# A four-layer NCHW network on one core: the queue of layer 0's image loads, the place of the second image's statistics, and the order of layer 3's scores

## The chip, the cores and the metric

The kernel runs on one core of one Trainium2 chip. The metric is the device time of the whole program in microseconds (us). Engines are named as the profile names them: PE (matrix multiply), DVE (vector), ACT (activations), POOL (GpSimd), SP (the engine that here only issues transfers). Each engine executes its own instructions in the order in which they were written for it, and instructions wait for each other across engines by semaphores. A transfer is issued by SP, ACT or POOL, and stands in that engine's queue like any other instruction.

## The reference, cut to what matters

All values are float32. The input x has 8 images of 384 channels on 32 x 32 pixels. Four layers follow each other, each as a residual on a group norm:

```python
def _gn(v, G=32, eps=1e-5):            # 12 channels per group
    g = v.reshape(B, G, C // G, H, W)
    m = g.mean((2, 3, 4), keepdims=True); s = g.var((2, 3, 4), keepdims=True)
    return ((g - m) / sqrt(s + eps)).reshape(v.shape)

# layer 0: three branches q, k, v of 3x3 depthwise conv, batch norm, gelu, 1x1 conv
def _dwproj(x, dw, g, b, pw):
    y = gelu(_bn(depthwise3x3(x, dw), g, b))        # _bn: moments over images and pixels
    return einsum('oc,bchw->bohw', pw, y)
# then attention of 8 heads over 1024 tokens, a 1x1 conv and a batch norm
x = x + layer0(_gn(x))
x = x + layer1(_gn(x))   # 4 experts of two 1x1 convs, each token with its best two
x = x + layer2(_gn(x))   # ternary 3x3 depthwise conv and 1x1 conv
x = x + layer3(_gn(x))   # attention of 6 heads from 1024 tokens to 256 sampled keys, then a 1x1 conv
...
# layer 3, for each head: scores, softmax over the 256 keys, weighted values
attn = softmax(einsum('bhqd,bhkd->bhqk', q, k) * SCALE)
out  = einsum('bhqk,bhkd->bhqd', attn, v)
```

## The kernel before, in words

**Layer 0's convolution stage** takes roughly the first 365 us of the program. An image lies on 128 partitions in 3 chunks of 1024 pixels, and arrives as 3 transfers of 512 KB (`load_x`, which calls `load_image`; its transfers are recorded at L169). Five image buffers are shared by the eight images x0 to x7. x0 is loaded through SP's queue, x1 and x2 through POOL's (x2 held behind a transfer of the first image's stacks), and x3 to x7 through SP's, each when the norm of the image before it begins.

**The norm of an image** (`norm(b)`) has three steps. `begin` runs six `bn_stats` over the image on DVE (L104, two for each chunk) and one aggregate (L109). `middle` is a small matmul that averages over the group (`gna`, L115), followed on DVE by `ga` (L117) and `dm` (L120). `end` is a second small matmul (`gnb`, L126), then `ve` on DVE (L128), a power of minus one half on POOL (L96), the shift `ss` on DVE (L131), and three activations on ACT (L145) that write the scaled image into one of two padded buffers, `pads[b % 2]`. For the images that `ON_V` names (0, 2, 4 and 6) a copy `xn` of the padded chunk follows on DVE (L277), and 27 depthwise taps of one part of the channels on DVE as well (L299, L301), with statistics and a transfer out at the end of each of the three branches (`finish`, L306 to L309, the transfer `raw<-yv` issued by ACT).

**The convolution on PE** goes by 60 groups of channels (`work`), in the order of the images. For each group SP builds a tile `st` with 3 transfers of 168 KB from the padded buffer (L327, three rows of taps side by side on the partitions, ten such buffers), up to nine groups ahead (`AHEAD`). PE then runs 12 matmuls into two accumulation banks (L414; four banks in all, which the small matmuls of the norm share). ACT copies each bank out (L420), DVE takes its statistics (L422), and ACT issues 3 transfers of the result `raw` to DRAM (L437). A norm's three steps are written before three consecutive groups, some groups ahead of the first group that needs the image.

The order within an engine is fixed when the kernel is built: a scheduler walks over the program by the order in which things were written and its own estimate of when they are ready. `tc.issue_after(x)` keeps what is written under it behind instruction x. Transfers issued by POOL share eight completion slots, those by SP and ACT eight others, so that a ninth transfer waits for the first of its kind to land.

**Layer 3's attention** runs over six units for each image (three pairs of heads, two halves of the tokens). For a unit, `scores` multiplies q and k in two blocks (`s`, L1666: PE writes two PSUM tiles of 128 x 1024, of which there are two in all), each followed by its exponential on ACT (`p`, L1673). POOL adds the two blocks of p (`p01`, L1718), `weigh` multiplies p with the values (`pav`, L1682), and `sums` multiplies `p01` of the unit before with ones (`pss`, L1695), by which `divide` divides on DVE. Before, the scores of unit u+1 are written at the end of unit u. Tiles `p` and `p01` come from one pool of five buffers (`pl.flat`). For all images but the last, matmuls of layer 1 for other images (`y`, L1367) are mixed in between the units on PE; the last image has none beside it. A final 1x1 conv (`pf`, L1782) ends each image.

Of the kernel before, what the change touches and what calls it, by code (L numbers as in the profile page):

```python
# [8 lines left out]
AF = mybir.ActivationFunctionType  # L9
# [3 lines left out]
B, C, H, W = 8, 384, 32, 32  # L13
N = H * W
P = 128
KC = C // P
# [5 lines left out]
GC, NGC, GR, BR = 42, 9, 6, 4  # L22
# [31 lines left out]
def tile_kernel(ctx: ExitStack, tc: tile.TileContext, i: dict, out: bass.AP):  # L54
    nc = tc.nc
# [9 lines left out]
    def big(name):  # L65
        return ps_big.tile([P, N], F32, tag="big", name=name)
# [32 lines left out]
    def gn_start(x, tag, c, st):  # L99

        if st is None:
            st = small.tile([P, 2 * KC, 6], F32, tag="gn_st", name=f"st_{tag}")
        for h in range(2):
            nc.vector.bn_stats(st[:, 2 * c + h, :], x[:, c, h * HALF : (h + 1) * HALF])  # L104
        return st
# [119 lines left out]
    with ExitStack() as pa:  # L225
# [9 lines left out]
        pads = []  # L235
# [6 lines left out]
        xts = {}  # L242

        def load_x(b, queue=nc.sync):
            xts[b] = image(f"xa{b}")
            return load_image(xts[b], x_img[b], queue)
# [7 lines left out]
        cwr = load_a("cwr")  # L254
        vst = wa.tile([3 * GC, 3, 2, 6], F32, name="vst")

        def norm(b):

            xt, state = xts.pop(b), {}

            def begin():
                st = None
                for c in range(KC):
                    st = gn_start(xt, f"a{b}", c, st)
                state["st"], state["mv"] = st, gn_mean(st, f"a{b}")

            def middle():
                state["dm"] = gn_spread(state["mv"], f"a{b}", bank)

            def end():  # L270
                ss = gn_scale(*state["dm"], f"a{b}", bank)
                for c in range(KC):
                    dst = pads[b % 2][:, c, 1 : H + 1, :]
                    affine(dst, xt[:, c, :].rearrange("p (h w) -> p h w", h=H), ss)
                if b in ON_V:
                    xn = wa.tile([3 * GC, H, W], F32, tag="xn", name=f"xn{b}", bufs=2)
                    nc.vector.tensor_copy(xn, pads[b % 2][: 3 * GC, KC - 1, 1 : H + 1, :])  # L277
                    taps.extend(convolve(b, xn))
                for c in range(KC):
                    moments(xmv[:, b, c, :], state["st"][:, 2 * c : 2 * c + 2, :])  # L280

            return [begin, middle, end]
# [79 lines left out]
        begins, n = {}, -3  # L362
# [6 lines left out]
        def stacks(n):  # L369
            while later and len(work) - len(later) < n and later[0][0] in normed:  # L370
                sts[later[0]] = stack(*later[0])
                later.pop(0)
# [17 lines left out]
        for n, (b, g) in enumerate(work):  # L390
            if n in begins:
                b2 = begins[n]
                for k, f in enumerate(norm(b2)):
                    todo[n + k] = f, (b2 if k == 2 else 0)
                if b2 + 1 < B and b2 + 1 not in xts:
                    load_x(b2 + 1)
            if n in todo:
                f, b2 = todo.pop(n)
                f()
                normed.add(b2)  # L400
            stacks(n + AHEAD + 1)
            st = sts.pop((b, g))
            nch = GC if g < NGC else GR * BR
            y = ya.tile([3 * nch, N], F32, tag="y", name=f"y{b}_{g}")
            pk = [bank(f"pk{b}_{g}_{h}") for h in range(2)]
            steps = [(h, k) for h in range(2) for k in range(3)]
            if g == NGC:
                stl = wa.tile([3 * GR * BR, 2, 6], F32, tag="stl", name=f"stl{b}")
            for h, k in steps:
                dx, c0, c1, o0 = TAPS[k]  # L410
                rows = slice(h * (H // 2), (h + 1) * (H // 2))
                lhs = cw[:, g, dx, :] if g < NGC else cwr[:, dx, :]
                rhs = st[:, rows, c0:c1]
                nc.tensor.matmul(  # L414
                    pk[h].rearrange("p (h w) -> p h w", w=W)[: 3 * nch, :, o0 : o0 + c1 - c0],
                    lhsT=lhs, rhs=rhs, start=(k == 0), stop=(k == 2),
                )
                if k == 2:
                    hs = slice(h * HALF, (h + 1) * HALF)
                    nc.scalar.copy(y[:, hs], pk[h][: 3 * nch, :])  # L420
                    st1 = cst[:, g, 2 * b + h, :] if g < NGC else stl[:, h, :]
                    nc.vector.bn_stats(st1, y[:, hs])  # L422
            for k in range(3 * BR if g == NGC else 0):

                (j, v), r = divmod(k, 3), k * GR
                b1 = b + 1 - BR + j
                nc.gpsimd.dma_start(out=raw[v][b1, 3 * GC :, :, :], in_=y[r : r + GR, :])
                if v == 0:
                    nc.gpsimd.dma_start(
                        out=cst[: 3 * GR, NGC, 2 * b1 : 2 * b1 + 2, :],  # L430
                        in_=stl[r : r + 3 * GR, :, :],
                    )
            for v in range(3 if g < NGC else 0):
                to, of = raw[v][b, g % 3 : 3 * GC : 3, g // 3, :], y[v : 3 * GC : 3, :]

                queue = nc.gpsimd if b == B - 1 and g in (5, 6, 7) else nc.scalar
                queue.dma_start(out=to, in_=of)  # L437
            for _ in range(2):
                if taps:
                    taps.pop(0)()  # L440
            if b == B - 1:
                if g == 5:
                    load_b(0)
                for k in () if g == NGC else (g, NGC) if g == 5 else (g,):
                    bn_moments(cst, k, bn0)
# [49 lines left out]
    scale = HD0 ** (-0.5)  # L495
# [757 lines left out]
    def third(pl, k, name):  # L1253

        return pl.one([P, KC, HALF], f"hd{k}", name)
# [205 lines left out]
    def layer3(pl, b, xt, put, general):  # L1461
# [195 lines left out]

        def scores(pr, h):

            ps = []  # L1660
            for kc in range(2):
                nm = f"3_{b}_{pr}_{h}_{kc}"
                s = big(f"s{nm}")
                for j in range(2):
                    r = slice(64 * j, 64 * j + 64)
                    nc.tensor.matmul(  # L1666
                        s[:, j * HALF : (j + 1) * HALF],
                        lhsT=kt[r, pr, kc * P : (kc + 1) * P],
                        rhs=q[r, pr, h * HALF : (h + 1) * HALF],
                        start=True, stop=True,  # L1670
                    )
                p = pl.flat([P, N], f"p{nm}")
                nc.scalar.activation(p, s, AF.Exp, scale=0.125)  # L1673
                ps.append(p)
            return ps

        def weigh(pr, h, ps):
            pav = vbank(f"pav3_{b}_{pr}_{h}")
            for kc in range(2):
                for j in range(2):  # L1680
                    hd = 2 * pr + j
                    nc.tensor.matmul(  # L1682
                        pav[64 * j : 64 * j + 64, :], lhsT=vt[:, kc, hd * 64 : (hd + 1) * 64],
                        rhs=ps[kc][:, j * HALF : (j + 1) * HALF],
                        start=(kc == 0), stop=(kc == 1),
                    )
            return pav


        if not general:  # L1690
            def sums(u, p01):

                pss = fbank(f"pss3_{b}_{u}")
                for j in range(2):
                    nc.tensor.matmul(  # L1695
                        pss[64 * j : 64 * j + 64, :], lhsT=ones[:, :64],
                        rhs=p01[:, j * HALF : (j + 1) * HALF], start=True, stop=True,
                    )
                return pss
# [11 lines left out]
                )  # L1711


            ps, due3 = scores(*units[0]), None
            yield UNIT
            for u, (pr, h) in enumerate(units):
                p01 = pl.flat([P, N], f"p01_{b}_{u}")
                nc.gpsimd.tensor_tensor(p01, ps[0], ps[1], ALU.add)  # L1718
                pav = weigh(pr, h, ps)
                if due3:  # L1720
                    pss = sums(due3[2], due3[4])

                tu = pl.one([P, NG * LS], f"om{u % 2}", f"tu_{b}_{u}")[:, :HALF]
                tu = tu.rearrange("p (a b) -> p a b", b=32)
                nc.vector.transpose(tu.rearrange("p a b -> p (a b)"), pav)
                if due3:
                    divide(pss, *due3[:4])
                due3 = pr, h, u, tu, p01
                if u + 1 < NU3:
                    ps = scores(*units[u + 1])  # L1730
                yield UNIT
                yield 0.0
            divide(sums(due3[2], due3[4]), *due3[:4])
# [285 lines left out]
```

## Time and profile before

| | |
|---|---|
| median of 3 runs | 3647.08 us (3642.57 to 3647.95) |
| the profiled execution's own time | 3643.82 us |
| its span, first to last instruction | 3641.9 us |
| PE busy | 3533.7 us, 97% of the span |
| DVE, ACT, POOL busy | 48%, 35%, 6% |
| mean granted PE clock | 0.984 of full speed |
| SP's queue | 206.53 MB, 16.9% of the transfer engines' time |
| ACT's queue | 37.19 MB, 3.0% |
| POOL's queue | 6.44 MB, 0.6% |

A line of a timeline gives the start in us, the duration in us, the engine, the line of the kernel, the operation, output and inputs with their sizes, the number of instructions merged (x3), and in brackets the engine's idle time just before, with what ended it. A line of a table of waits gives the waiting engine and line, what it waited for, the total in us, how often, and the longest. A table by windows gives for each stretch each engine's busy time with its instructions, then the granted PE clock (1.00 is full speed), the share of the 16 transfer engines in use and the GB/s that they moved.

### The profile page before, as it was taken

Reading aid. Unit: us, or ns where it says so; the run is one execution under the profiler, and the core shown is the slowest. Engines: PE = TensorE matmul, PEld = TensorE weight load, DVE = VectorE, ACT = ScalarE, POOL = GpSimd, SP = SyncE. Lnnn points to the kernel's source line nnn. Section 1 sums busy time; section 2 is a strip of 40 time slices with the busy share of each in tenths; the row PEclk is TensorE's granted clock in tenths of the full one; section 3 lists DMA queues with packets and bytes.
Section 4 is the critical chain, followed back from the end, with each engine's and each line's share of the span. In section 5 each row is a group of like instructions: output and inputs, shape, how many; then the busy total and the mean of one; then the engine's idle time right before and its main releaser. Section 6 shows DMA issues by size and latency. Waiting matters only on the chain.

```text
span 3641.9 us, 38824 instructions
## 1 busy us (share of the span) xinstructions
PE 3533.7 (97%) x15533; PEld 1537.9 (42%) x15533; DVE 1752.0 (48%) x2808; ACT 1267.4 (35%) x1512; POOL 218.1 (6%) x201
## 2 busy tenths in 40 slices
PE   7999999999999999999899999999999999999888
PEld 3444343434343434344344444445344444444434
DVE  6776123232323232323346556374664647556663
ACT  2232554444444445434212321323322232322222
POOL 1101100000000000000000010200102010010112
PEclk9999999999999999999999999999999999999898
DMA  7767211111202020212430010111101001010000
GB/s 252 239 233 271 72 57 37 66 54 51 73 29 77 26 76 26 76 28 76 181 149 29 28 52 21 39 49 34 38 24 56 26 34 44 28 52 21 0 35 18
DMA packets 88893, 252.78 MB, mean 69 GB/s; under 512 B 19774, under 2 KB 20438, under 8 KB 88318
## 3 DMA queue, kind: packets, MB, share of 16 engines
q1 hardware_dynamic: 73972, 206.53, 16.9%
q10 hardware_dynamic: 12120, 37.19, 3.0%
q0 software_dynamic: 2608, 6.44, 0.6%
q8 instruction: 127, 2.08, 0.2%
q14 instruction: 66, 0.54, 0.1%
HBM read 133.44 MB, written 75.59 MB: 57 GB/s over the span
## 4 chain that ended last, share of the span: by engine, by line
PE 47%; DVE 2%; ACT 1%; POOL 1%; issue 0%; DMA 0%; DVEq 0%; POOLq 0%; ACTq 0%
PE ph L1346 14%; PE y L1367 14%; PE pq L1487 3%; PE pw L1450 3%; PE pf L1782 3%; PE s L1666 2%; PE pav L1682 2%; PE pk L1640 1%; PE pss L1695 1%; PE pv L1649 1%; PE xsb L1626 1%; PE plog L1096 1%; DVE off L1557 1%; DVE y L1442 1%; POOL p L1718 1%; ACT p L1673 1%
## 5 line engine op out<-in xcount | busy, mean ns | idle before, releaser
L696 ACT ACTIVATE p<-s 128x1024 f32<-128x1024 f32 x512 | 496.4, 1021 | 371.6 <-PE s L689 371.3
L704 PE MATMUL pav<-p,vt 64*64 64x512 f32 x4096 | 495.5, 589 | 0.0
L1367 PE MATMUL y<-hd,w_sb 128*128 128x512 f32 x1080 | 488.6, 600 | 3.5 <-DVE hd L1332 3.5
L1346 PE MATMUL ph<-h,w_sb 128*128 128x512 f32 x1104 | 485.2, 595 | 0.1
L689 PE MATMUL s<-qk,qk 48*64 48x512 f32 x3072 | 370.7, 593 | 0.0
L414 PE MATMUL pk<-st,cw_sb 126*126 126x512 f32 x720 | 314.7, 598 | 12.3 <-DMA st<-pad 11.6
L1346 PEld LDWEIGHTS ph<-h,w_sb 128*128 128x128 f32 x1104 | 208.0, 190 | 258.9 <-issue 255.1
L1367 PEld LDWEIGHTS y<-hd,w_sb 128*128 128x128 f32 x1080 | 200.2, 191 | 246.5 <-issue 236.0
L704 PEld LDWEIGHTS pav<-p,vt 64*64 64x64 f32 x4096 | 171.4, 133 | 270.6 <-issue 266.7
L665 DVE COPY ta<-pav 128x512 f32<-128x512 f32 (+1 forms) x65 | 44.2, 682 | 475.3 <-PE pav L704 475.3
L1442 DVE SCALAR_TENSOR_TENSOR y<-h,tap,y 128x961 f32<-128x961 f32 (+1 forms) x192 | 233.5, 1239 | 0.6
L1356 ACT ACTIVATE hd<-ph,b_sb 128x512 f32<-128x512 f32 x180 | 122.6, 681 | 311.1 <-PE ph L1346 311.1
L414 PEld LDWEIGHTS pk<-st,cw_sb 126*126 126x126 f32 x720 | 137.9, 193 | 178.4 <-issue 175.1
L1557 DVE SCALAR_TENSOR_TENSOR off<-q,dw_sb,off 128x225 f32<-128x225 f32 (+3 forms) x432 | 212.2, 546 | 1.6
L689 PEld LDWEIGHTS s<-qk,qk 48*64 48x64 f32 x3072 | 113.3, 133 | 220.7 <-issue 199.1
L79 DVE COPY qk<-pq 128x512 f32<-128x512 f32 x48 | 33.2, 692 | 265.4 <-PE pq L604 265.4
L1673 ACT ACTIVATE p<-s 128x1024 f32<-128x1024 f32 x96 | 93.2, 1021 | 189.3 <-PE s L1666 189.2
L420 ACT COPY y<-pk 126x512 f32<-126x512 f32 (+1 forms) x124 | 70.4, 584 | 227.2 <-PE pk L414 112.0
L1332 DVE TENSOR_TENSOR hd<-hd,cb 128x512 f32<-128x512 f32 x180 | 122.2, 684 | 41.1 <-ACT hd L1356 40.8
L1718 POOL TENSOR_TENSOR p<-p,p 128x1024 f32<-128x1024 f32 x48 | 113.0, 2354 | 369.1 <-ACT p L1673 369.1
L1782 PE MATMUL pf<-att,wp_sb 128*128 128x512 f32 x288 | 130.0, 607 | 4.3 <-DVE att L1709 3.7
L604 PE MATMUL pq<-g,wq_sb 128*128 128x512 f32 x288 | 129.7, 601 | 2.5 <-DMA wq_sb<-in_wq_dram 2.5
(296 smaller groups left out, 3856.2 us busy)
## 6 DMA issues: line engine op xcount, KB each, us to landing
g<-raw SPq DMA_DIRECT2D x72, 512.0 KB
st<-pad SPq DMA_DIRECT2D x180, 168.0 KB
raw<-y ACTq DMA_DIRECT2D x171, 168.0 KB
xh<-in_x_dram SPq DMA_DIRECT2D x48, 256.0 KB
f<-in_x_dram SPq DMA_DIRECT2D x24, 512.0 KB
f<-o SPq DMA_DIRECT2D x24, 512.0 KB
o<-ot SPq DMA_DIRECT2D x42, 256.0 KB
x<-in_x_dram SPq DMA_DIRECT2D x21, 512.0 KB
```

Of the source, the lines that this page charges most:

```text
L414: nc.tensor.matmul(pk[h].rearrange("p (h w) -> p h w", w=W)[: 3 * nch, :, o0 : o0 + c1 - c0], lhsT=lhs, rhs=rhs, start=(k == 0), stop=(k = ...
L604: nc.tensor.matmul(pq, lhsT=w_in[v][:, c, pr * P : (pr + 1) * P], rhs=acts[b][v][:, c, h * HALF : (h + 1) * HALF], start=(c == 0), stop=(c ...
L689: nc.tensor.matmul(s[64 * k : 64 * k + 64, j * HALF : (j + 1) * HALF], lhsT=kt[r, k0 : k0 + 64], rhs=qt[r, h * HALF : (h + 1) * HALF], sta ...
L696: nc.scalar.activation(p, s, AF.Exp, scale=scale)
L704: nc.tensor.matmul(pav[k][64 * j : 64 * j + 64, :], lhsT=vts[b % 2][r, kc, 2 * hd : 2 * hd + 2, :].rearrange("p a b -> p (a b)"), rhs=p[r, ...
L1346: nc.tensor.matmul(ph, lhsT=w1[:, e, c, dc * P : (dc + 1) * P], rhs=state["h1"][c], start=(c == 0), stop=(c == KC - 1),)
L1367: nc.tensor.matmul(y, lhsT=w2[:, e, dc, m * P : (m + 1) * P], rhs=state[h, k], start=(k == 0), stop=(k == NE * KC - 1),)
L1442: nc.vector.scalar_tensor_tensor(d, f, tap2[:, c, t : t + 1], d, ALU.mult, ALU.add)
L1557: nc.vector.scalar_tensor_tensor(d, f, dw3[:, t : t + 1], d, ALU.mult, ALU.add)
L1673: nc.scalar.activation(p, s, AF.Exp, scale=0.125)
L1718: nc.gpsimd.tensor_tensor(p01, ps[0], ps[1], ALU.add)
L1782: nc.tensor.matmul(pf[:, hs], lhsT=wp3[:, pr, m * P : (m + 1) * P], rhs=att[:, pr, hs], start=(pr == 0), stop=(pr == NPAIR3 - 1),)
```

## The change

There are three parts. The first writes the six statistics of image 1 (`begin` of `norm(1)`) under `issue_after` of image 0's copy `xn`, so that they stand behind it on DVE. The second takes the loads of x3 to x7 off SP's queue, and issues each on POOL's queue, in the text of the program right behind the `end` of the norm of the image before. The third splits layer 3's `scores` in its matmuls (`scores`) and its exponentials (`exps`): the matmuls of unit u+1 are written ahead of the `weigh` of unit u, and the exponentials behind `weigh` and `sums`; for the last image the exponentials too stand ahead of `weigh`, and their outputs lie in other tiles (`third`, four tiles, `hd0` to `hd3`, that layers 1 and 2 use earlier).

```diff
+        first_pad = []
         def norm(b):
             xt, state = xts.pop(b), {}
             def begin():
                 st = None
-                for c in range(KC):
-                    st = gn_start(xt, f"a{b}", c, st)
+                with tc.issue_after(first_pad[0].ins) if b == 1 else nullcontext():
+                    for c in range(KC):
+                        st = gn_start(xt, f"a{b}", c, st)
...
-                    nc.vector.tensor_copy(xn, pads[b % 2][: 3 * GC, KC - 1, 1 : H + 1, :])
+                    first_pad.append(
+                        nc.vector.tensor_copy(xn, pads[b % 2][: 3 * GC, KC - 1, 1 : H + 1, :])
+                    )
...
-                if b2 + 1 < B and b2 + 1 not in xts:
-                    load_x(b2 + 1)
             if n in todo:
                 f, b2 = todo.pop(n)
                 f()
                 normed.add(b2)
+                if 1 < b2 < B - 1:
+                    load_x(b2 + 1, nc.gpsimd)
...
         def scores(pr, h):
-            ps = []
+            ss = []
             for kc in range(2):
-                nm = f"3_{b}_{pr}_{h}_{kc}"
-                s = big(f"s{nm}")
+                s = big(f"s3_{b}_{pr}_{h}_{kc}")
...
-                p = pl.flat([P, N], f"p{nm}")
-                nc.scalar.activation(p, s, AF.Exp, scale=0.125)
+                ss.append(s)
+            return ss
+
+        def exps(u, ss):
+            ps = []
+            for kc in range(2):
+                nm = f"p3_{b}_{u}_{kc}"
+                if last:
+                    p = third(pl, 2 * (u % 2) + kc, nm).rearrange("p a n -> p (a n)")[:, :N]
+                else:
+                    p = pl.flat([P, N], nm)
+                nc.scalar.activation(p, ss[kc], AF.Exp, scale=0.125)
                 ps.append(p)
             return ps
...
-            ps, due3 = scores(*units[0]), None
+            ps, due3 = exps(0, scores(*units[0])), None
             yield UNIT
             for u, (pr, h) in enumerate(units):
                 p01 = pl.flat([P, N], f"p01_{b}_{u}")
                 nc.gpsimd.tensor_tensor(p01, ps[0], ps[1], ALU.add)
+                nxt = scores(*units[u + 1]) if u + 1 < NU3 else None
+                if last and nxt:
+                    nxt = exps(u + 1, nxt)
                 pav = weigh(pr, h, ps)
                 if due3:
                     pss = sums(due3[2], due3[4])
+                if nxt:
+                    ps = nxt if last else exps(u + 1, nxt)
...
-                if u + 1 < NU3:
-                    ps = scores(*units[u + 1])
                 yield UNIT
```

## The prediction

> **What bounds the kernel now.** First the page: PE is busy for 97% of the span, so only its gaps can be won. Then the chain that ended last and the groups: nothing but PE carries weight. So the table of PE's waits up to 460 us, then the timelines around the gaps.
>
> ```profile
> PE 3533.7 (97%) x15533; PEld 1537.9 (42%) x15533; DVE 1752.0 (48%) x2808; ACT 1267.4 (35%) x1512; POOL 218.1 (6%) x201
> ```
>
> The table of waits names the engine and line, what it waited for, the sum in us, how often, and the longest:
>
> ```profile
> PE gna_a L115 <- DVE mv_a L109: 16.8, 3, 9.1
> PE pk L414 <- DMA st<-pad: 11.6, 1, 11.6
> PE pmove L466 <- DVE rest L460: 5.3, 1, 5.3
> PE gna_a L115 <- DVE xmv L142: 3.6, 1, 3.6
> ```
>
> The convolution stage waits in two places: at the start for the first stacks, later for statistics of images (5.42 us at 175.99, 2.31 at 257.55, and 3.58 at 85.39; the 9.1 is the first image's load, which stays).
>
> ```profile
> 11.15 0.56 POOL L96 TENSOR_TENSOR ss_a<-ve_a,mhalf 128x1 f32<-128x1 f32 x1 [2.19 <-DVE ve_a L128]
> 11.79 1.28 DVE L104 BATCH_NORM_STATS2 st_a<-xa 128x6 f32<-128x512 f32 x2 [0.71 <-DMA xa<-in_x_dram]
> ...
> 16.19 0.10 DVE L131 SCALAR_TENSOR_TENSOR ss_a<-ga_a,ss_a 128x1 f32<-128x1 f32 x1
> 16.33 3.50 ACT L145 ACTIVATE pad<-xa,ss_a 128x1024 f32<-128x1024 f32 x3 [10.42 <-DVE ss_a L131]
> ...
> 22.46 6.07 PE L414 MATMUL pk<-st,cw_sb 126*126 126x512 f32 x9 [11.59 <-DMA st<-pad]
> ```
>
> And of PE alone at the later gaps:
>
> ```profile
> 85.39 0.56 PE L115 MATMUL gna_a<-mv_a,g_sb 128*128 128x2 f32 x2 [3.58 <-DVE xmv L142]
> 85.81 8.06 PE L414 MATMUL pk<-st,cw_sb 126*126 126x512 f32 x12
> ...
> 175.99 0.56 PE L115 MATMUL gna_a<-mv_a,g_sb 128*128 128x2 f32 x2 [5.42 <-DVE mv_a L109]
> ```
>
> POOL's power is done at 11.71, but the shift `ss` comes at 16.19: image 1's six statistics stand between, and everything of image 0 hangs on it. The group after the gap at 85.39 takes 8.06 us, where one takes 5.1 later.
>
> ```profile
> 40.00:50.00 10.00, 9.52 (x23) 4.07 (x22) 5.08 (x9) 4.41 (x7) 0.00 (x0) 1.00 0.92 319
> 60.00:85.00 25.00, 21.82 (x52) 9.43 (x51) 20.08 (x28) 7.81 (x12) 0.00 (x0) 0.99 0.83 282
> 85.00:90.00 5.00, 4.61 (x7) 2.27 (x8) 4.22 (x10) 0.00 (x0) 0.00 (x0) 0.50 0.73 251
> ```
>
> These windows show transfer engines at 0.92 while x2 loads, at 0.83 later, and PE's clock at 0.50 after the gap.
>
> **What the Trainium skill says.** "TensorE: Matmul & The Clock Gate", section "What's actually happening": after an idle window of about 3.4 us PE runs at half clock for about as long. The trace agrees: 0.50, and 8.06 - 5.1 = 3.0 us lost; the groups behind the gaps at 175.99 and 257.55 took 7.15 and 6.98, so 2.1 and 1.9 lost. "DMA: Bandwidth & Descriptors", section "Queues, rings and completion order": each transfer engine goes round its queues packet by packet, so another queue shares bandwidth and adds none. In the first window three queues add up to 319 GB/s at 0.92, 347 at most, which fits. "Perfetto Trace Analysis", section "DMA Instruction — SWDGE (GPSIMD)": what the profile shows on POOL is the making of descriptors, not the moving. x2's three take 1.63 us from 37.02, and DVE sees the data at 42.91, 45.89 and 48.38: it agrees.
>
> **Part 1, the statistics of image 1.** `ss` moves from 16.19 to about 11.8, behind POOL's power: -4.4 us for the scaled image, `st`, PE's first group and everything up to group 5. The 4.3 us of statistics are now behind the copy `xn` (19.87 + 0.69, less 4.4), where DVE idles 6.55 us before 27.91: cost nothing; without that cover 4.3 us of DVE ahead of taps that nobody waits for.
>
> **Part 2, the loads.** 15 issues leave SP, 15 join POOL. SP's slots are cheap there (stacks are issued 5 to 8 us ahead of PE in groups 3 to 8). On POOL nothing is queued but the powers of the norms. But the built order differs from the text: nothing ties a load to the norm it is written behind, and POOL's queue reads ss_a1, x2, x3, x4, x5, two chunks of x6, and only then the power of image 2, the third chunk, x7. All are asked for from 37.02 - 4.4 = 32.6 us on, at POOL's 0.54 us each (1.63 / 3); x5 needs x0's buffer (free by then), x6 x1's (free at about 37), and at most eight are in flight. DVE follows: image 2's `dm` stands behind the statistics of x4's second chunk's first half, its `ve` behind x5's first chunk, its `ss` behind x5's second, image 3's `ve` behind x7.
>
> So the time of one load, r, decides. Bounds: x1 alone moved at 281 GB/s (5 us of the trace), 524 KB in 1.9 us; x2 beside SP's 82 and ACT's 34 GB/s got 214, 2.45 us; DVE saw it every 2.7. I take 2.4: PE will stall here, and a stalled PE asks for less. Then, with landings at 38.5, 41.5, 44.0 (before, less 4.4) and each r later:
> - x4's second chunk lands at 44 + 5 x 2.4 = 56.0, `dm` of image 2 at 57.0; PE reaches `gnb` at 56.2 - 4.4 = 51.8: 5.3 us idle, some 2 of slow clock.
> - x5's second chunk lands at 63.2, with 1.3 of statistics `ss` comes at 64.6 (before 57.46). ACT's three activations and the copy queued behind them end at 70.2, PE's group 8 waits for that bank (before 66.1).
> - DVE's taps of image 2's part end at 86.9 (before about 72), since statistics stand among them. ACT's transfer of that result waits, and holds the bank copies queued behind it to 90.1; PE's group 11 is held there.
> - `ve` of image 3 is made at 101.8, `ss` at 103.4 (before 96.88), ACT's scaling ends at 108.7, and group 14 starts at 109.3 (before 103.6), some 2 of slow clock with it: +5.7 + 2 = +8 us against before, part 1's gain and the loss of 6.6 at 85.39 counted in.
>
> Images 5 and 7 are in their buffers long before their norms: -(5.42 + 2.1) - (2.31 + 0.65 + 1.9) = -12.4. Parts 1 and 2 together -4.4. The same replay gives +3.3 at r = 1.9, so 9.4 us for each us of r, and +9.9 at 2.75; above that I keep 9.4, since 8 loads after x2 stand ahead of image 2's `ss` and 15 ahead of image 3's `ve`.
>
> **Part 3, layer 3.** A unit of images 0 to 5 takes 7.4 us on PE (scores 1.92, fill of layer 1 2.77, values 1.87, sums 0.86) and has no gap except at the last unit, 0.27 and 0.49 an image. Scores earlier, exponentials later: the second exponential now waits for a buffer that `pss` frees; ACT's two take 2 x 1.02 us under 2.77 of fill. I take 0, bounds -2 and +4 with the stretch from 3440 to 3545 us, where DVE leads. The last image has no fill:
>
> ```profile
> 3588.93 1.08 PE L1682 MATMUL pav<-p,vt 128*64 128x512 f32 x4 [1.50 <-ACT p L1673]
> ...
> 3594.30 1.08 PE L1682 MATMUL pav<-p,vt 128*64 128x512 f32 x4 [0.32 <-ACT p L1673]
> ...
> 3617.85 1.08 PE L1695 MATMUL pss<-p,ones 128*64 128x512 f32 x4 [0.49 <-POOL p L1718]
> ```
>
> Its gaps are 1.50 + 2 x 0.32 + 0.27 + 2 x 0.26 + 0.49 = 3.4. With scores a unit ahead each exponential has 1.87 more to hide in; only the last sum on POOL (2.35) stays: -2.8.
>
> **The sum.** -4.4 + 0 - 2.8 = -7.2 us on the profiled execution's 3643.8: 3636.6. That execution was 3.3 below the median of 3647.08, so the forecast for the median is 3639.9, rounded 3640. What a measurement can tell from no change here is about 0.2%, 7.3 us: it sits on that edge.
>
> **Rivals.**
> (a) Loads faster, or DVE's statistics never late. At 281 GB/s the sum is +3.3 - 12.4 - 2.8 = -12: 3635. If no new wait appears at all, 4.4 + 12.4 + 2.8 = 19.6 are gained: 3627. For it: 281 was measured. Against: stacks and results were not moving then.
> (b) The reverse: POOL's queue gets the leavings. The window from 60 to 85 moved 282 GB/s at 0.83, so 340 in full; a group's six transfers of 172 KB in 5.1 us need 202, which leaves 138, and r = 3.8; three queues that all have work and share evenly leave 113, and r = 4.6. The sum passes zero at 2.4 + 7.2 / 9.4 = 3.2 us a load (165 GB/s), is slower by 7.3 from 3.95 on, and at 4.3, between the two, stands at +10.7: 3658. For it: SP, without image loads in its queue, runs ahead and asks for more. Against: PE's own stalls cut that demand.
> (c) No difference: r between 2.7 and 3.9 gives back at 50 to 110 us what images 5 and 7 return, 3643 to 3654, as r = 3.2 gives 3647. The place of the loads in the text would make no difference.
> (d) The scores of unit u+1 hold PSUM tiles that the fill wants, or wait for ACT: up to +4 in part 3, on top of any of these.
>
> **How the numbers follow.** My own case 0.36 (own range 3632 to 3648, half of it on each side of the edge), (a) 0.23, (b) 0.25, (c) with (d) 0.16. Faster 0.18 + 0.23 = 0.41; same 0.18 + 0.16 = 0.34; slower 0.25. The range leaves out the far end of (a) and the worst of (b): 3629 to 3659.
>
> **What would show it.** Step 1: `ss` of image 0 near 11.8, PE's first group near 18. Step 2: on POOL fifteen transfers ahead of image 2's power; DVE seeing a load every 2.4 us; PE idle 5 us before image 2's `gnb`; no wait at images 5 and 7. Part 3: no wait of `pav` in the last image. The forecast is wrong if r is far from 2.4, if PE waits for `st` between 40 and 90 us (stacks crowded out), or if layer 3's units grow beyond 7.4 us.

## The result, and the profile after

| | before | after |
|---|---|---|
| median | 3644.54 us (3638.92 to 3649.73, 15 runs) | 3636.39 us (3632.90 to 3639.65, 15 runs) |
| span of the profiled execution | 3641.9 us | 3634.6 us |

The ratio of after to before is 0.9976, with a 95% interval of 0.9969 to 0.9982: about 8.7 us faster (6.6 to 11.3). The forecast was 7.2 us. The two profiled executions differ by 7.3 us. PE is as full as before, and the fifteen transfers moved from SP to POOL show in POOL's count of instructions (201 before, 216 now). The page's first part, of the changed kernel:

```profile
PE 3528.1 (97%) x15533; PEld 1531.5 (42%) x15533; DVE 1766.5 (49%) x2808; ACT 1269.3 (35%) x1512; POOL 225.5 (6%) x216
```

Where PE waited in the first 460 us of the changed kernel (engine and line, what it waited for, sum in us, times, longest):

```profile
PE gna_a L115 <- DVE mv_a L109: 9.5, 2, 9.0
PE pk L421 <- DMA st<-pad: 9.4, 3, 7.6
PE gnb_a L126 <- DVE dm_a L120: 8.8, 2, 8.1
PE pmove L473 <- DVE rest L467: 5.3, 1, 5.3
PE pk L421 <- DVE ga_a L117: 3.0, 3, 2.5
```

The wait for the first stacks fell from 11.6 to 7.6 us. The waits of images 5 and 7 for their statistics are gone from the first line (16.8 before; of the 9.5 that stay, 9.0 are the first image's load and 0.5 image 2's). In their place stands a wait of 8.1 us for image 2's `dm`.

The timeline of the changed kernel's start:

```profile
11.07 0.56 POOL L96 TENSOR_TENSOR ss_a<-ve_a,mhalf 128x1 f32<-128x1 f32 x1 [2.13 <-DVE ve_a L128]
11.67 0.16 DVE L131 SCALAR_TENSOR_TENSOR ss_a<-ga_a,ss_a 128x1 f32<-128x1 f32 x1 [0.68 <-POOL ss_a L96]
11.86 3.50 ACT L145 ACTIVATE pad<-xa,ss_a 128x1024 f32<-128x1024 f32 x3 [6.03 <-DVE ss_a L131]
15.40 0.69 DVE L282 COPY xn<-pad 126x1024 f32<-126x1024 f32 x1 [3.57 <-ACT pad L145]
16.01 3.65 DVE L104 BATCH_NORM_STATS2 st_a<-xa 128x6 f32<-128x512 f32 x6
18.42 2.04 PE L421 MATMUL pk<-st,cw_sb 126*126 126x512 f32 x2 [7.63 <-DMA st<-pad]
```

The shift is made 0.04 us after POOL's power, image 1's six statistics run behind `xn` with nobody waiting, and PE's first group starts at 18.42 where it started at 22.46.

POOL's own timeline shows the hoisted loads:

```profile
32.80 4.22 POOL L169 DMA_DIRECT2D xa<-in_x_dram  x8
39.81 0.53 POOL L169 DMA_DIRECT2D xa<-in_x_dram  x1 [2.79 <-DMA xa<-in_x_dram]
43.72 0.53 POOL L169 DMA_DIRECT2D xa<-in_x_dram  x1 [3.38 <-DMA xa<-in_x_dram]
46.30 0.53 POOL L169 DMA_DIRECT2D xa<-in_x_dram  x1 [2.06 <-DMA xa<-in_x_dram]
49.19 0.53 POOL L169 DMA_DIRECT2D xa<-in_x_dram  x1 [2.36 <-DMA xa<-in_x_dram]
52.97 0.53 POOL L169 DMA_DIRECT2D xa<-in_x_dram  x1 [3.25 <-DMA xa<-in_x_dram]
56.24 0.53 POOL L169 DMA_DIRECT2D xa<-in_x_dram  x1 [2.75 <-DMA xa<-in_x_dram]
66.56 0.56 POOL L96 TENSOR_TENSOR ss_a<-ve_a,mhalf 128x1 f32<-128x1 f32 x1 [9.79 <-DVE ve_a L128]
```

Eight loads go out at once, and each further one when one has landed. So this queue is a clock for landings: 39.81 to 56.24 is 5 landings, 3.3 us each. Image 2's power comes only at 66.56, behind fourteen loads. It did not wait for them in POOL's queue: DVE made the `ve` that it needs at 66.27. What is late is DVE.

The table by windows shows the transfer engines meanwhile (the last two numbers are their share in use and the GB/s):

```profile
40.00:56.00 16.00, 12.05 (x29) 4.83 (x27) 9.26 (x20) 1.75 (x3) 2.45 (x5) 1.00 1.03 354
56.00:62.00 6.00, 0.00 (x0) 0.00 (x0) 4.56 (x13) 1.07 (x2) 0.53 (x1) 0.81 0.95 380
```

They are full, and stay so while PE stands still.

PE's timeline of the changed kernel, first where image 2 waits, then at the first small matmuls of images 4 and 5:

```profile
62.45 0.59 PE L126 MATMUL gnb_a<-dm_a,g_sb 128*128 128x1 f32 x2 [8.15 <-DVE dm_a L120]
...
147.34 0.28 PE L115 MATMUL gna_a<-mv_a,g_sb 128*128 128x2 f32 x2
...
178.42 0.28 PE L115 MATMUL gna_a<-mv_a,g_sb 128*128 128x2 f32 x2
```

Image 4's first small matmul stood at 139.32 before: 8.0 us late. Image 5's stood at 175.99 behind a gap of 5.42; now there is no gap, and 2.4 us are left of the delay. Matmul by matmul, the rest of the account of the two profiled executions is: -4.9 us at the end of the convolution stage (`pmove` 366.99 to 362.12), kept until layer 1; back to -1.9 after layer 3's images 0 to 5 (at 3440 us); -3.8 at the sampling of the last image (3564.35 to 3560.51); -8.8 at its final 1x1 conv (3618.86 to 3610.07); and -7.3 at the end of the program, since 8.7 us pass from the last matmul to the end where 7.2 passed before.

All this is one execution of each kernel, and executions of one and the same code spread. Four traces have the old convolution stage (the kernel before and three of the experiments): image 4's first small matmul stands in them at 138.7 to 142.7, and `pmove` at 367.0 to 371.2. The changed stage has a second trace below, with 150.4 and 365.2. A difference of 4 us between two single traces of this stage is therefore no finding by itself.

The last image, changed kernel, PE's timeline:

```profile
3583.95 2.04 PE L1672 MATMUL s<-q,kt 64*128 64x512 f32 x8 [1.21 <-ACT p L1689]
...
3610.07 2.41 PE L1801 MATMUL pf<-att,wp_sb 128*128 128x512 f32 x5
```

From the first unit's scores to the final conv there is one wait, 1.21 us, before the second unit's scores, and no other.

### The profile page after: what moved, and what is told of

It is laid out like the page before. It is cut to its first block, busy times and chain, and to the rows that moved or that the text cites. A ratio compares the mean times of both kernels' runs of the same rounds, so it can differ in the third digit from the quotient of the medians.

```text
span 3634.6 us, 38829 instructions
## 1 busy us (share of the span) xinstructions
PE 3528.1 (97%) x15533; PEld 1531.5 (42%) x15533; DVE 1766.5 (49%) x2808; ACT 1269.3 (35%) x1512; POOL 225.5 (6%) x216
## 4 chain that ended last, share of the span: by engine, by line
PE 40%; DVE 9%; ACT 1%; DMA 1%; POOL 0%; issue 0%; DVEq 0%; ACTq 0%; POOLq 0%
PE y L1374 11%; PE ph L1353 9%; DVE y L1449 5%; PE pq L1494 3%; PE pw L1457 3%; PE pf L1801 3%; PE s L1672 2%; PE pav L1698 2%; DVE hd L1339 1%; PE pk L1647 1%; PE pv L1656 1%; DMA o<-o 1%; PE pss L1711 1%; PE xsb L1633 1%; PE plog L1103 1%; DVE off L1564 1%
## 5 line engine op out<-in xcount | busy, mean ns | idle before, releaser
L1457 PE MATMUL pw<-y,upw 128*128 128x512 f32 x288 | 130.0, 605 | 4.1 <-DVE y L1449 4.1
```

The lines of the kernel that those rows point to most:

```text
L1457: nc.tensor.matmul(pw[h], lhsT=upw2[:, c, m * P : (m + 1) * P], rhs=y[c][:, hs], start=(c == 0), stop=(c == KC - 1),)
```

## The experiments

The theory to test was the forecast's own: the three parts add up, part 2 costs early what it returns late, because statistics that wait for hoisted loads stand in front of the norms on DVE. All differences below are (ratio - 1) times some 3644 us, with the interval of the ratio.

**Each part alone.**

Part 1 and part 2 alone are the diffs shown above without the other parts.

> The kernel before with part 1 alone (image 1's statistics behind the copy xn). My theory: the stage starts 4.4 us earlier and nothing takes it back, -4.4 us (-3.5 to -5). Rival, part 1 is absorbed: the wait of PE at 85 us ends with the load of x3 on SP's queue, and if that load does not come earlier the wait grows by what the start gained: 0, and the gap before image 3's first small matmul grows from 3.6 to about 8.

Measured: ratio 0.9988 (0.9982 to 0.9995), -4.4 us (-6.6 to -1.8). The gap before image 3's small matmul is 3.4 us in its trace (3.6 before), so nothing is taken back there: the load of x3 on SP's queue comes earlier as well, since what stands ahead of it in that queue does. The rival falls.

> The kernel before with part 2 alone (x3 to x7 on POOL's queue). My theory: the late norms of images 2 and 3 cost about what images 5 and 7 return, 0 us (-2 to +3): a wait of 5 to 8 us before image 2's second small matmul, some 12 us behind by 130 us, even by 270 us. Rival, the loads carry the whole gain of the change: -8 us.

Measured: ratio 1.0000 (0.9992 to 1.0009), 0 us (-2.9 to +3.3). In its trace image 4 is 16 us late, and 3 us are left at the end of the stage. Part 2 by itself buys nothing.

> The kernel before with part 3 alone. My forecast: -2.8 us, all of it in the last image. From the trace of the changed kernel: the last image gains 4.9, images 0 to 5 lose about 3, the stretch before the last image returns 1.8: -2 to -4. Rival, layer 3's order does nothing to the time: 0.

Measured: ratio 1.0003 (0.9995 to 1.0011), +1.1 us (-1.8 to +4.0). The expected -2.8 lies outside the interval. In the trace the last image gains 4.2 us from its sampling to its final conv, the part of the program before it loses 3.0, and 1.3 us are left. PE's waits between 2000 and 3300 us in this kernel:

```profile
PE ph L1346 <- ACT h L1295: 5.4, 5, 1.5
PE pw L1450 <- DVE y L1442: 0.9, 5, 0.2
```

and in the kernel before:

```profile
PE pss L1695 <- POOL p L1718: 3.0, 6, 0.5
PE pav L1682 <- ACT p L1673: 1.6, 6, 0.3
```

The old waits at the end of each image are gone, 4.6 us. In their place come 6.3 us: a pair of layer 1's matmuls (`ph`) has been scheduled one step earlier, ahead of the scaled image that ACT makes for it, and waits 5.4 us, and the matmuls of `pw` wait 0.9.

Part 3 for the last image alone:

```diff
-                nxt = scores(*units[u + 1]) if u + 1 < NU3 else None
-                if last and nxt:
-                    nxt = exps(u + 1, nxt)
+                nxt = None
+                if last and u + 1 < NU3:
+                    nxt = exps(u + 1, scores(*units[u + 1]))
...
                 due3 = pr, h, u, tu, p01
+                if not last and u + 1 < NU3:
+                    ps = exps(u + 1, scores(*units[u + 1]))
```

> The kernel before with part 3 for the last image alone; for images 0 to 6 scores and exponentials stand where they stood before. If the new order costs images 0 to 5 some 3 us, this is faster than part 3 alone by about 3, at -5 us. Rival, the loss seen there belongs to the layers' other waits and would come anyway: the same as part 3 alone, within 1 us.

Measured: ratio 0.9992 (0.9986 to 0.9999), -2.9 us (-5.1 to -0.4). This is the forecast's -2.8 for the last image, and by the medians 4 us better than part 3 for all images, though the two intervals overlap a little.

**Parts 1 and 2 together.**

> Parts 1 and 2 together, layer 3 as before. If the parts simply add, -4.4 + 0 = -4.4 us, as part 1 and part 2 alone measured. If part 1 and part 2 need each other, the changed kernel's -8.7 less part 3's +1: about -9 to -10.

Measured: ratio 0.9989 (0.9981 to 0.9997), -4.0 us (-6.9 to -1.1). The first two parts add. What does not add is the third: -4.0 and +1.1 make -2.9, and the changed kernel has -8.7 (-11.3 to -6.6). With the intervals that is a difference of 5.8 us, uncertain by nearly as much. In the traces layer 3 is worth 3.9 us in the changed kernel and 1.3 alone; the waits of `ph` differ, 3.8 us against 5.4.

The traces of all runs, those further below with them, settle more than these two. This is the stretch from `pmove` to PE's last matmul, which parts 1 and 2 leave as it is, in us against the kernel before (the sampling begins with the last image's first `xsb`):

| | `pmove` to the last image's sampling | from there to its final conv | whole stretch |
|---|---|---|---|
| without part 3 (4 more traces) | -1.1 to 0.0 | 0.0 to +0.3 | -1.1 to 0.0 |
| part 3 for all images (5 traces) | +1.0 to +3.0 | -4.2 to -5.0 | -1.3 to -3.9, median -2.9 |
| part 3 for the last image alone (4 traces) | -0.1 to +1.4 | -4.1 | -2.7 to -4.2, median -4.0 |

So part 3 for all images gains in all five kernels that have it: 1.3 us alone, 2.4 to 3.9 beside the other parts. With it for the last image alone the gain is about 1 us larger, not 4. The 5.8 us between the measured times are more than this explains; the rest stays open.

**Is it the order on DVE, or the traffic?** First the loads tied to the norm that they are written behind:

```diff
     def rsqrt(dst, var, n):
-        nc.gpsimd.tensor_tensor(dst, var, mhalf[: var.shape[0], :n], ALU.pow)
+        powers.append(nc.gpsimd.tensor_tensor(dst, var, mhalf[: var.shape[0], :n], ALU.pow))
...
                 if 1 < b2 < B - 1:
-                    load_x(b2 + 1, nc.gpsimd)
+                    with tc.issue_after(powers[-1].ins):
+                        load_x(b2 + 1, nc.gpsimd)
```

> The changed kernel, with each image's loads held behind the power of the norm before it on POOL, so that POOL's queue reads as the text does and x3 is asked for behind image 2's power, x4 behind image 3's, and so on. My theory, DVE's queue full of statistics that wait for hoisted loads is what costs 12 us at 50 to 110 us: no wait before image 2's second small matmul, none at images 3, 5 and 7, so 4.4 + 6.6 + 12.4 less some 3 for DVE waiting a load's 5 us behind each shift, and part 3's +1: -19 us (-15 to -23). Rival, loads on POOL's queue beside the stacks are slow wherever they stand, and hold up the stacks: no more than the -8.7 of the change.

Measured: ratio 0.9976 (0.9970 to 0.9983), -8.7 us (-10.9 to -6.2): the time of the changed kernel, and less than half of what was expected. Its trace on PE:

```profile
52.71 0.28 PE L128 MATMUL gnb_a<-dm_a,g_sb 128*128 128x1 f32 x2
...
65.50 15.37 PE L424 MATMUL pk<-st,cw_sb 126*126 126x512 f32 x36 [2.31 <-DMA st<-pad]
...
133.26 0.28 PE L117 MATMUL gna_a<-mv_a,g_sb 128*128 128x2 f32 x2
...
170.03 0.56 PE L117 MATMUL gna_a<-mv_a,g_sb 128*128 128x2 f32 x2 [5.54 <-DVE mv_a L111]
```

The wait at image 2 is gone, and image 4 comes at 133.26, 6.1 us before the old kernel and 14.1 before the changed one. But image 5 waits 5.54 us again. Its norm follows image 4's by some 30 us, its load was asked for only behind image 4's power at 142.5, and DVE took from 149.9 to 169.6 to get through its statistics between taps. Tying removed the early cost and brought the late one back. Another 2.0 us went at 322 us, where PE waited for ACT.

Then the opposite, loads as early as in the changed kernel, but the statistics of images 3 to 7 held on DVE:

```diff
-                with tc.issue_after(first_pad[0].ins) if b == 1 else nullcontext():
+                held = first_pad[0] if b == 1 else shifts[-1] if b > 2 else None
+                with tc.issue_after(held.ins) if held else nullcontext():
```

where `shifts` collects the shift `ss` of each norm (L131).

> The changed kernel with its early loads left as they are, but the statistics of images 3 to 7 held on DVE behind the shift of the image before. My theory, the order on DVE is the cause and the traffic is not: nearly as good as tying the loads, with image 2's power behind two chunks of x6 on POOL as the only rest, some 4 to 8 us: -11 to -17 us. Rival, the early traffic itself is the cost: stays at -8.7, with PE waiting for stacks instead.

Measured: ratio 0.9971 (0.9960 to 0.9981), -10.6 us (-14.6 to -6.9). Just outside what the theory allowed, with the rival's sign in the trace:

```profile
55.19 0.28 PE L128 MATMUL gnb_a<-dm_a,g_sb 128*128 128x1 f32 x2
...
70.06 18.14 PE L424 MATMUL pk<-st,cw_sb 126*126 126x512 f32 x36 [4.39 <-DMA st<-pad]
...
141.57 0.28 PE L117 MATMUL gna_a<-mv_a,g_sb 128*128 128x2 f32 x2
```

Image 2 does not wait. PE does, for a stack: 4.39 us, and the 36 matmuls behind, at half clock at first, take 18.14 us for 15.37 in the tied kernel. Is that traffic? From 40 to 56 us the transfer engines are full here and not in the tied kernel. First this kernel, then the tied one:

```profile
40.00:56.00 16.00, 13.73 (x36) 6.12 (x35) 9.54 (x22) 2.12 (x4) 2.65 (x5) 1.00 1.02 348
40.00:56.00 16.00, 15.44 (x41) 7.00 (x40) 9.29 (x23) 4.07 (x6) 2.14 (x4) 1.00 0.85 283
```

And the stack came late because it was asked for late. SP could not issue it before one of the eight slots that SP and ACT share came free, and that slot was held by ACT's transfer of DVE's own result, `raw<-yv`. In this kernel the transfer is issued at 51.03, and SP goes on at 61.10, 10.1 us later (a line of the table of SP's waits, then two of the timeline):

```profile
SPq L336 <- DMA raw<-yv: 2.8, 1, 2.8
51.03 0.39 ACTq L316 DMA_DIRECT2D raw<-yv  x1
61.10 9.58 SPq L336 DMA_DIRECT2D st<-pad  x8
```

In the tied kernel the same two stand at 47.71 and 53.54, 5.8 us apart:

```profile
47.71 0.79 ACTq L315 DMA_DIRECT2D raw<-yv  x1
53.54 16.67 SPq L335 DMA_DIRECT2D st<-pad  x13
```

So of the 14.1 us between the changed and the tied kernel at image 4, holding DVE's order returns 5.8 (147.34 to 141.57), and only taking the early traffic away returns the other 8.3 (to 133.26). Both causes are real. Which is the larger is not shown: these are single traces that spread by up to 4 us, and the traffic's cost came out only once DVE's order no longer covered it.

The tied loads with part 3 for the last image alone:

> Loads held behind each norm's power, and part 3 for the last image alone. The two add: the tied kernel less about 4 us, -23 us (-19 to -27). Rival, the layer 3 parts differ by noise: the same as the tied kernel within 1 us.

Measured: ratio 0.9975 (0.9966 to 0.9985), -9.1 us (-12.4 to -5.5). No more than the tied kernel; the loss of part 3 in images 0 to 5 does not show here.

**A version that pays neither.** x3 behind image 2's power, x4 and x5 behind image 3's, x6 and x7 behind image 4's, DVE's statistics held as above, part 3 for the last image alone:

```diff
-                if 1 < b2 < B - 1:
-                    load_x(b2 + 1, nc.gpsimd)
+                for b3 in {2: (3,), 3: (4, 5), 4: (6, 7)}.get(b2, ()):
+                    with tc.issue_after(powers[-1].ins):
+                        load_x(b3, nc.gpsimd)
```

> Loads on POOL held behind powers, but with time to land: x3 behind image 2's, x4 and x5 behind image 3's, x6 and x7 behind image 4's; statistics of images 3 to 7 held on DVE behind the shift of the image before; part 3 for the last image alone. If early traffic (8 us between the held and the tied kernel at 139 us) and DVE's order (6 us between the changed and the held one) are the two costs, and late loads the reason for the tied kernel's stall at image 5, this pays none of them: -6 by image 4's first small matmul as in the tied kernel, then -12.4 for images 5 and 7, -18 at the end of the stage, and -2.9 for the last image: -21 us (-17 to -24). Rival, something takes the gain back that the traces do not show, as in the tied kernel, where -19 became -9: not below -12.

Measured: ratio 0.9961 (0.9948 to 0.9975), -14.2 us (-19.0 to -9.1), median 3630.90 us: the fastest kernel of the study, though short of the -21 expected, and its interval overlaps the changed kernel's. PE's waits for image data, up to 460 us:

```profile
PE gna_a L119 <- DVE mv_a L113: 9.0, 1, 9.0
PE pk L427 <- DMA st<-pad: 8.5, 2, 7.5
...
PE gnb_a L130 <- DVE dm_a L124: 3.1, 2, 2.5
PE pk L427 <- DVE ga_a L121: 2.2, 3, 1.7
```

Only the first image's two waits are long. In this trace the stage ends 13.8 us earlier than before, not 18: at image 5 PE waits 2.5 us for the `dm` that DVE makes between its taps, and the 96 matmuls behind take 42.20 us for 40.59. The 1.7 us for `ga` are image 3's, as in the tied kernel (1.41).

With part 3 for all images instead:

> As the spread kernel, with part 3 for all images. If the scores ahead cost images 0 to 5 some 3 to 5 us (early matmuls of layer 1 that wait for ACT) and the stretch before the last image returns 2 to 3, this is 1 to 3 us slower than the spread kernel. Rival: the same within 1 us, or faster, as the changed kernel against parts 1 and 2 alone (-4) would say.

Measured: ratio 0.9972 (0.9960 to 0.9984), -10.2 us (-14.6 to -5.8). Slower than the spread kernel by 4 us, with intervals that overlap. In two pairs of three the last image alone was better by 4 in the median, in one the same. But in the traces of this last pair 4.5 us arise in the convolution stage, where both kernels have the same code (`pmove` at 353.20 and 357.65), and only 1.2 behind it. So part 3 is best kept to the last image, for the 1 us of the table above; the 4 is not shown to come from it.

**The end of the program.** The account above lost 1.5 us behind the last matmul. The last long instruction on POOL is a drain, by line (count, shortest, median and longest in ns, from and to). Before:

```profile
L2015 POOLq DRAIN  x3: 46/107/3981, 3637.1 to 3641.7; - x3
```

After:

```profile
L2034 POOLq DRAIN  x3: 50/107/5206, 3628.6 to 3634.4; - x3
```

3.98 us with 48 transfers issued by POOL, 5.21 with 63: 0.083 us a transfer in both. To test it, 64 transfers of no use:

```diff
+                if pr == 1 and h == 0 and b == 4:
+                    probe = const.tile([P, 64], F32, name="probe")
+                    for k in range(64):
+                        nc.gpsimd.dma_start(out=probe[:, k : k + 1], in_=atts[3][:, 0, k : k + 1])
```

> The kernel before with 64 extra transfers of 128 x 4 bytes on POOL's queue in the middle of layer 0's attention, where POOL does nothing; what they move is used by nothing. The traces so far end with one instruction on POOL that took 3.98 us in the kernels with 48 transfers on that queue and 5.21 us in those with 63, 0.083 us a transfer. If that is a cost of every transfer POOL ever issued, it takes 112 x 0.083 = 9.3 us here and the program ends 5.3 us later: +5.3 (+4 to +6.5). Rival, the instruction is long for another reason, or only under the profiler: 0.

Measured: ratio 1.0014 (1.0006 to 1.0021), +5.1 us (+2.2 to +7.7).

```profile
L2019 POOLq DRAIN  x3: 50/107/9207, 3640.7 to 3650.5; - x3
```

9.21 us for 112 transfers. The rate holds, the program ends later by it, and not under the profiler alone. And with fewer:

```diff
-                nc.gpsimd.dma_start(out=raw[v][b1, 3 * GC :, :, :], in_=y[r : r + GR, :])
+                nc.sync.dma_start(out=raw[v][b1, 3 * GC :, :, :], in_=y[r : r + GR, :])
...
-                    nc.gpsimd.dma_start(
+                    nc.sync.dma_start(
                         out=cst[: 3 * GR, NGC, 2 * b1 : 2 * b1 + 2, :],
```

> The spread kernel with 32 of POOL's other transfers (the last channels' results and statistics) on SP's queue: 31 transfers are left on POOL. If each costs 0.083 us at the end, POOL's last instruction takes 2.6 us and no longer ends after SP's wait for the output: 1.2 to 1.6 us faster than the spread kernel, so -15 to -16. Rival, the transfers on SP hold up the stacks: slower than the spread kernel, with a wait for a stack at 140 or 265 us.

Measured: ratio 0.9983 (0.9977 to 0.9990), -6.2 us (-8.4 to -3.6), 8 us slower than the spread kernel's -14.2. The drain did what the rate says:

```profile
L2042 POOLq DRAIN  x3: 46/107/2592, 3631.1 to 3635.6; - x3
```

2.59 us for 31 transfers, and 7.2 us from the last matmul to the end as in the kernel before. But PE's table of waits has a new first line:

```profile
PE pmove L479 <- DVE rest L473: 16.2, 1, 16.2
```

That wait was 5.3 us. The rival was right that SP's queue is no free place, and wrong about where. DVE waits at the end of the stage for statistics of its own part of the channels, which SP transfers too (`cst<-vst`):

```profile
DVE bnmv_qkv L159 <- DMA cst<-vst: 10.1, 1, 10.1
```

Ahead of these statistics SP's queue had stood for 9.9 us, again for a slot that a `raw<-yv` kept; in the spread kernel it waits for none there. Whether the moved transfers made that one slow was not followed.

## Why the prediction was right, step by step

The time, 3636.4 for a forecast of 3640 within 3629 to 3659, follows from a sum whose order of events was right, and whose totals were partly right by errors that met. Of the 3.5 us between forecast and result, 2.5 are its base: the median of three runs before was 3647.08, that of fifteen 3644.54.

- **Part 1.** `ss` at 11.67 for 11.8, PE's first group at 18.42 for "near 18", -4.4 alone for -4.4. The cover held.
- **Part 2, the order.** POOL's queue, DVE's statistics and image 2's power stood where the working put them: fourteen loads ahead of the power, as its list of the queue adds up to (its "fifteen" is a slip). Rival (c)'s "the place of the loads in the text would make no difference" is answered in part: the tied kernel moved image 4 by 14 us, and then lost it elsewhere, so that its time is the changed kernel's.
- **Part 2, the time of a load.** 2.4 us was assumed. It was 3.3 at first (39.81 to 56.24), then 2.2 (five landings, 55.98 to 66.81), and 2.6 on average from x2's last chunk (46.04) to x5's second. PE's stall did not empty the transfer engines, as the working supposed: they were 0.95 in use from 56 to 62 us, and moved 380 GB/s, more than the 347 that it took for the most. The steps came late by this: `dm` at 62.26 for 57.0, the stall 8.15 for 5.3, `ss` at 68.01 for 64.6, image 3's `ss` at 106.33 for 103.4. Yet image 4 was +8.0 for +8, since two errors met: group 14 started at 111.93 for 109.3, but behind a wait of 1.88 us its matmuls ran at full clock, and the 2 us of slow clock that the sum had there did not come.
- **Part 2, the cause.** The working charged all of the early loss to the queues of DVE and ACT. The held and the tied kernel show both DVE's order (5.8 us) and traffic (8.3): a result that takes 10.1 us for 5.8 keeps a slot, and the next stack with it. "The Trainium skill", page "DMA: Bandwidth & Descriptors", section "Queues, rings and completion order", which says that each transfer engine serves its queues in turn, was used by the forecast for the time of a load. It holds for SP's and ACT's transfers as well, and the runs agree: engines 1.02 in use with early loads, 0.85 without. Rival (b), crowded stacks, was a right mechanism at a smaller price, hidden behind the wait at image 2. The sign that the forecast had named for it, PE waiting for `st` between 40 and 90 us, is in the changed kernel's trace, but small: 1.4 and 0.4 us.
- **Images 5 and 7.** From +8.0 at image 4 to -4.8 behind image 7's second small matmul, 12.8 returned for 12.4. One reading behind this was loose. The forecast said that the trace agrees with its page on the clock, half speed after an idle window of about 3.4 us and for about as long. The half clock is there, but in the kernel before it began within the gaps of 3.58 and 5.42 and lasted 6.8 us, 6.0 and 4.2 of them behind the gap, and it came for 3.4 us behind one of 2.31 too.
- **Part 3, images 0 to 5.** Taken as 0 between -2 and +4; they lost 3.0, in part by layer 1's matmuls moved ahead of ACT's scaling (3.8 us of waits for the 4.6 that went), a wait the working did not name. The stretch before the last image returned 1.9.
- **Part 3, the last image.** Forecast -2.8, in the trace -4.9 with the sampling before it. The waits fell from 3.4 to 1.2 us, and not to the 0.6 supposed, but a unit took 4.64 us for 5.04 where its idle time had been 0.26 to 0.32, and the sampling took 0.9 us less. These two are measured and not explained. Timed alone, part 3 for the last image was worth -2.9.
- **The end.** +1.5 us that no step had: fifteen more transfers on POOL, at 0.083 us each, in the drain.

-4.9 + 3.0 - 1.9 - 4.9 + 1.4 = -7.3 in the traces, for -4.4 + 0 - 2.8 = -7.2. Faster was the likeliest of the forecast's three outcomes, at 0.41, and the range was wide. That the total of one pair of traces came within 0.1 of the sum was luck: +1.1 and +1.4 us that it did not have stand against -2.1 more in the last image and -0.5 more in the convolution stage. Part 3 for all images comes to a median of -2.9 in five traces, so its -2.8 was right as a total.

## What to carry to other kernels

With a scheduler that orders by readiness, code written behind something is not issued behind it: a load without an input goes as early as its queue allows, and takes its consumers' places in other queues with it. When loads are moved earlier, price the traffic that they displace as well as the queues that they stand in, since a stall of the consumer can hide the displaced transfers. A slow transfer also keeps a slot that another queue's next transfer needs: here a result of ACT held up a stack of SP. Where an order helps only the stretch that has nothing else to run, give it only to that stretch. And before a difference between two traces is explained, look at how far apart two traces of the same code are.

## What the runs showed of the hardware that was not expected

The program's last drain on POOL took 0.083 us for every transfer that POOL had issued since the start: 2.59 us for 31, 3.98 for 48, 5.21 for 63, 9.21 for 112. In the kernel before it ended together with SP's wait for the output and cost nothing; each transfer beyond 48 then made this program 0.083 us longer, whether of 512 bytes or of 512 KB.

PE's clock fell to half also behind some gaps of less than 3 us, and not behind others of the same length. Behind 2.31 us of idle time in the kernel before and 2.47 in the spread kernel it fell, for 3.4 us; behind 2.31 in the tied kernel and 2.53 in the changed one it stayed full. At five longer gaps in the convolution stage (3.58 and 5.42 in the kernel before, 8.15 in the changed one, 4.39 in the held and 5.54 in the tied) it was half for 6.8 us, twice that; the half clock began within the gap, so that 3.6 to 6.0 us of it fell on the matmuls behind. What decides was not found. The stretches at the gaps of 3.58 and 2.31 us in the kernel before, by windows (the third number from the end is the granted clock):

```profile
84.58:91.41 6.83, 6.02 (x9) 2.94 (x10) 5.99 (x12) 0.20 (x1) 0.00 (x0) 0.50 0.74 257
258.66:262.08 3.42, 3.42 (x6) 1.36 (x5) 3.42 (x6) 0.19 (x1) 0.00 (x0) 0.50 0.73 247
```
